# Four layers on one core, the last a mixture of experts: adds of two parts declared free of each other, weights kept, one list moved to the end

## The chip, the core and the metric

The kernel runs on one core of a Trainium2 chip. The metric is the device time of one execution in microseconds (us). Six kinds of engine matter here. TensorE (PE) multiplies matrices and turns tiles; VectorE (DVE), ScalarE (ACT) and GpSimd (POOL) compute on tiles; SyncE (SP) issues nearly all plain DMA transfers, from one queue, in order; GpSimd issues the indirect ones, which write rows to places that a list of numbers gives. Sixteen DMA engines move the data. Each engine works through its own instructions in the order in which the program emits them, and waits at an instruction until what it needs is there.

## What is computed

The input `x` has 16 sequences of 256 tokens of 256 numbers, in float32; `ctx` has the same shape. Four layers follow each other, each adding to `x`:

```
x = x + cross_attention_8_heads(ctx, layernorm(x))      # layer 1: keys from both, 512 of them
x = x + ffn_with_token_products(layernorm(x))           # layer 2: 1024 hidden, gelu
x = x + cross_attention_1_head(layernorm(x), ctx)       # layer 3
y = layernorm(x)                                        # layer 4: mixture of 8 experts
w = routing_weights(y @ Wr / temperature)               # 8 weights per token, some are 0
x = x + sum over e of w[e] * (silu(y @ Wg[e]) * (y @ Wu[e])) @ Wd[e]
```

An expert's three weights have 256 x 256 numbers each. A token counts for an expert only if its weight there is not 0.

## The kernel before

**Head loop.** The outer loop has 128 steps `n`, one for each head of each sequence (8 heads by 16 sequences), and two more to empty the pipeline. Step `n` computes scores `sc` (`s1`), then `pq` and `pk` of the next head, some filling work (`bulk`: values `pv`, the next sequence's input, and in the first sequence the loads of `load_late`), the product `po` of head `n-2` (`s3`), and the turning of the probabilities of head `n` (`s2`). The turning goes through memory: VectorE turns 32 x 32 blocks into `tb`, SyncE sends `tb` to a buffer `hop` in DRAM (L831) and, when that has landed, reads it back in another order as `pT` (L834). So `pT` of a head has to be back when `po` comes up two steps later.

**Chains.** What follows the first layer for one sequence is a generator, `chain`: output projection `px`, layer 2 (`ph`, `pf`), layer 3, and the last layernorm. Then `route` finds each token's experts and writes each row of the sequence into 8 lists in DRAM, `slots_d`, by 16 indirect DMAs on GpSimd (L638).

**Experts.** The sequences are split in two parts, of 9 and 7, so that the experts can start on the first part before the last sequences are done. A list of part 0 has 9 tiles of 128 rows for each expert, a list of part 1 has 7. They are worked in groups of 3, 3, 3 and of 4, 3 tiles (4, 2, 1 for the very last list): first all eight lists of part 0, then all eight of part 1. A group's rows are loaded from its list (L1040), turned through DRAM (L290, L296) into `yTd`, multiplied with the gate and up weights (`pg`, `pu`), and, in the midst of the next group, with the down weights (`pd`). VectorE scales each tile's result into `o` (8 buffers, L1122), and GpSimd adds it to the rows of the output in DRAM by an indirect DMA with addition (L1123). Rows of one list go to different places, so the adds of one list are declared free of each other by `apart`; adds of different lists wait for each other. A group's rows are loaded three groups ahead. For a group of part 1 that waits until `route` of the last sequence is through (the `ready` test).

**Weights.** `load_expert` loads the three weights of the expert two groups ahead (L1022 to L1024), into one of two buffers in turn, for each list anew: 16 loads.

**The order of the work** around the change is made by a planner at build time. `Clock.pe` is its estimate of TensorE's time; each matmul that is emitted moves it on. Chains, routes and experts are jobs in `line`; a job's `yield 2.5` says that its next unit is ready 2.5 us of clock later. Between the stages of the head loop, `gap` emits units of the first ready job until 0.8 us of clock are filled, and returns at once if no job is ready. After the head loop a last loop lets the clock jump to the next ready job until all are done.

**Memory.** Pools are opened and closed as stacks: `work_a` holds the head loop's tiles and `Wo_sb` to the end; `work_d`, the experts' tiles, is opened in the last step but two.

Of the kernel before, what the change touches and what calls it, by code (L numbers as in the profile page):

```python
# [12 lines left out]
F32 = mybir.dt.float32  # L13
# [16 lines left out]
def xattn_ffn_kernel(  # L30
# [74 lines left out]

    def apart(ins, group):
        tc.declare_no_dep(
            ins.ins, group=group, reason="rows of one group go to different places"  # L110
        )
        tc.add_to_no_dep_group(group, ins.ins)
        nc.gpsimd.nop()

    def gap(least=0.8):

        t = Clock.pe
        while Clock.pe - t < least:
            line[:] = [j for j in line if not j.done]
            job = next((j for j in line if j.ready <= Clock.pe), None)  # L120
            if job is None:
                return
            job.unit()
        line[:] = [j for j in line if not j.done]

# [529 lines left out]

    wh = ctx.enter_context(tc.tile_pool(name="work_a", bufs=2))
    with ExitStack() as sa, ExitStack() as sf:
        wi = sa.enter_context(tc.tile_pool(name="work_i", bufs=2))  # L660
        wf = sf.enter_context(tc.tile_pool(name="work_f", bufs=2, side="right"))

# [275 lines left out]
        def load_late(h):  # L938
            if h == 0:
                nats["W2"] = load_turn(W2, DC, HC, "W2e")  # L940
            if h == 1:
                nats["Wv"] = load_turn(Wv_w, DC, DC, "v1")
                nats["qk"] = load_fold()
            if h == 2:
                nc.sync.dma_start(Wo_sb, Wo.rearrange("(h p) d -> p h d", p=P))
                nc.sync.dma_start(Wr_sb, Wr.rearrange("(c p) e -> p c e", p=P))
                lasting["b2"] = row_everywhere(b2, "b2_bc")
                lasting["bv1"] = row_everywhere(Wv_b, "bv1_bc")
                lasting["scale"] = row_everywhere(ffn_scale, "scale_bc")
                lasting["invt"] = row_everywhere(temperature, "temp_bc")  # L950
            if h == 4:
                nc.vector.reciprocal(lasting["invt"], lasting["invt"])

        def all_turns():
# [49 lines left out]
        class D_:  # L1004


            w, wk = {}, None


        def open_front():  # L1010
            D_.front = ctx.enter_context(tc.tile_pool(name="front_d", bufs=2, side="right"))

        def open_last_layer():
            D_.wk = ctx.enter_context(tc.tile_pool(name="work_d", bufs=2))

        def load_expert(key):
            e = key[1]
            k = len(D_.w) % 2
            w = D_.w[key] = (D_.wk if k else D_.front).tile(
                [P, 3, DC, D], F32, tag=f"wx{k}", bufs=1, name=f"wx_{key[0]}_{e}"  # L1020
            )
            nc.sync.dma_start(w[:, 0], Wg[e].rearrange("(c p) i -> p c i", p=P))  # L1022
            nc.sync.dma_start(w[:, 1], Wu[e].rearrange("(c p) i -> p c i", p=P))
            nc.sync.dma_start(w[:, 2], Wd[e].rearrange("(c p) d -> p c d", p=P))  # L1024

        class G:


            def __init__(self, part, e, t0, tiles, more):
                self.part, self.e, self.tiles = part, e, tiles  # L1030
                self.key = (f"{part}{more}", e)
                self.name = f"{part}_{e}_{t0}"
                self.first = e * NTOKS[part] + t0 * P

# [45 lines left out]

            def gate(self, i):
                n = self.tiles * P
                w = D_.w[self.key]
                if i == 0:
                    self.hT = D_.wk.tile(
                        [P, IC, n], F32, tag="hTd", name=f"hTd_{self.name}",
                        padded_shape=[P, IC, NG],
                    )
                self.pg = mm_tile(n, f"pg_{self.name}_{i}")
                for d in range(DC):  # L1090
                    mm(
                        self.pg, w[:, 0, d, ts(i, P)], in_order(self.yT)[:, d],
                        start=(d == 0), stop=(d == DC - 1),
                    )
                self.sg = D_.wk.tile(
                    [P, n], F32, tag="sg", name=f"sg_{self.name}_{i}", padded_shape=[P, NG]
                )
                nc.scalar.activation(self.sg, self.pg, AF.Tanh, scale=0.5)  # L1098

            def up(self, i):  # L1100
                w, sg = D_.w[self.key], self.sg
                pu = mm_tile(self.tiles * P, f"pu_{self.name}_{i}")
                for d in range(DC):
                    mm(
                        pu, w[:, 1, d, ts(i, P)], in_order(self.yT)[:, d],
                        start=(d == 0), stop=(d == DC - 1),
                    )
                nc.vector.scalar_tensor_tensor(sg, sg, 1.0, self.pg, ALU.add, ALU.mult)
                nc.vector.tensor_tensor(self.hT[:, i, :], sg, pu, ALU.mult)  # L1109

            def down(self, t):
                if t >= self.tiles:
                    return
                w = D_.w[self.key]
                pd = mm_tile(D, f"pd_{self.name}_{t}")
                for i in range(IC):
                    mm(
                        pd, self.hT[:, i, ts(t, P)], w[:, 2, i, :],
                        start=(i == 0), stop=(i == IC - 1),
                    )  # L1120
                o = D_.wk.tile([P, D], F32, tag="o", bufs=8, name=f"o_{self.name}_{t}")
                nc.vector.tensor_scalar(o, pd, self.wt[:, t : t + 1], None, ALU.mult)  # L1122
                ins = nc.gpsimd.indirect_dma_start(  # L1123
                    out=out_rows[0 : sum(NTOKS[: self.part + 1]), :],
                    out_offset=bass.IndirectOffsetOnAxis(ap=self.at[:, t : t + 1], axis=0),
                    in_=o, in_offset=None, compute_op=ALU.add,
                )
                apart(ins, f"out_{self.part}_{self.e}")

        def experts(groups, ready=None):  # L1130

            load_expert(groups[0].key)
            for g in groups[:2]:
                g.load()
            yield 7.0
# [6 lines left out]
            for n, g in enumerate(groups):  # L1142
                if n == 0:
                    groups[2].load()
                if n + 3 < len(groups):
                    while ready is not None and not ready(groups[n + 3]):
                        yield 0.4
                for i in range(IC):
                    g.gate(i)
                    yield  # L1150
                    g.up(i)
                    yield
                    if n == 0:
                        groups[1].turn_rows(i)
                    if n + 2 < len(groups):
                        if i == 0:
                            groups[n + 2].send_rows()
                        else:
                            groups[n + 2].fetch_rows()
                    if i == 0 and n + 3 < len(groups):  # L1160
                        groups[n + 3].load()
                    if late is not None:
                        late.down(2 * i)
                        late.down(2 * i + 1)
                        yield
                if n + 2 < len(groups) and groups[n + 2].key not in D_.w:
                    load_expert(groups[n + 2].key)
                late = g
            for t in range(late.tiles):
                late.down(t)  # L1170

        def groups(part, more, sizes, last_sizes=None):

            gs = []
            for e in range(E):
                t = CAPS[part] // P if more else 0
                for k in last_sizes if last_sizes and e == E - 1 else sizes:
                    gs.append(G(part, e, t, k, more))
                    t += k
                assert t == NTOKS[part] // P if more else t == CAPS[part] // P  # L1180
            return gs

        last = None
        for n in range(NS + 2):
# [6 lines left out]
            if n == NS - 4:  # L1191
                sf.close()
                open_front()
                rest = Job(experts(
                    groups(0, "", (3, 3, 3)) + groups(1, "", (4, 3), (4, 2, 1)),
                    lambda g: g.part == 0 or last.tail.done,
                ))
                line.append(rest)
# [2 lines left out]
                open_last_layer()  # L1201
            while behind_exp:
                behind_exp.pop()()
            gap()
            if n < NS:
                s1_scale(n)
            if n + 1 < NS:
                s0q(n + 1)
            gap()
            if n + 1 < NS:  # L1210
                s0k(n + 1)
            gap()
            advance(more)
            gap()
            advance(more)
            gap()
            if n >= 2:
                s3(n - 2)
            gap()
            if n < NS:  # L1220
                s2(n)
        line.remove(rest)
# [2 lines left out]
        while line:  # L1225
            while behind_exp:
                behind_exp.pop()()
            if not any(j.ready <= Clock.pe for j in line):
                Clock.pe = min(j.ready for j in line)
            gap()  # L1230


        more_d = keep.tile([P, 2, E], F32, name="more_d")
# [46 lines left out]
```

## Time and profile before

| what | value |
|---|---|
| median of 3 runs | 1898.36 us (1895.84 to 1899.13) |
| the profiled execution, its own time | 1899.3 us |
| its span | 1897.6 us |
| TensorE busy (matmul) | 1845.4 us, 97% |
| VectorE, ScalarE, GpSimd busy | 1179.6, 594.8, 872.3 us |
| mean granted TensorE clock | 0.991 |
| bytes moved by DMA | 309.89 MB, 163 GB/s |
| GpSimd's adds to the output (L1123) | 128, 1562 ns each |
| GpSimd's writes of slots (L638) | 256, 1050 ns each |
| matmuls of the experts pg, pu, pd | 127.6, 125.3, 123.8 us |
| last layer's groups, first pg to last pd | 1477.7 to 1877.9 us |

The span is the time from the first to the last recorded instruction; the execution's own time is 1.7 us longer. Busy time of one engine can lie beside that of another, so the shares don't add up to one. In the lines of the timelines that follow, the first number is the start in us from the start of the span, the second the duration, then the engine, the source line, the operation and the tiles (what is written <- what is read), how many instructions are merged in the line, and in brackets how long the engine had been idle before and what ended that. Matmuls overlap by a fraction of a microsecond, so the start of the next line says more than the end of one.

### The profile page before, as it was taken

To read this page: it belongs to the slowest core of one execution; us is meant where nothing else is said; L and a number is where in the kernel's file an instruction comes from. 1 tells how busy PE (TensorE), PEld (TensorE's weight loads), DVE (VectorE), ACT (ScalarE), POOL (GpSimd) and SP (SyncE) were. 2 spreads that over 40 slices of the span, in tenths; PEclk is the share of its full clock that TensorE was granted. 3 is DMA by queue.
4 is the path that set the end of the run, shared out by engine and by line. 5 is a ranking of instruction groups with operands and counts; after the bars stand their busy time and mean duration, and the time that the engine had idled before them with its cause. 6 is when DMAs were issued, how large, how long until landed. Compare 5 with 4: busy or idle time off the path is not lost.

```text
span 1897.6 us, 22669 instructions
## 1 busy us (share of the span) xinstructions
PE 1845.4 (97%) x6822; PEld 1252.6 (66%) x6822; DVE 1179.6 (62%) x3211; ACT 594.8 (31%) x1309; POOL 872.3 (46%) x996
## 2 busy tenths in 40 slices
PE   8999999999999999999999999999999999999995
PEld 4566666666666666666666666667676767665554
DVE  5356667666666666666675766666657476656553
ACT  3333434343333333333333333333333221111110
POOL 3122353535353535353534444444434367766565
PEclk9999999999999999999999999999999999999998
DMA  6553445454545444444454444444435477999995
GB/s 217 160 170 103 161 137 159 141 166 138 162 140 159 148 151 157 151 147 149 146 160 151 149 154 143 159 140 160 142 118 177 135 200 194 250 234 241 249 220 96
DMA packets 235083, 309.89 MB, mean 163 GB/s; under 512 B 27036, under 2 KB 195912, under 8 KB 232904
## 3 DMA queue, kind: packets, MB, share of 16 engines
q1 hardware_dynamic: 204184, 256.80, 43.2%
q0 software_dynamic: 30720, 51.54, 11.5%
q8 instruction: 57, 0.93, 0.2%
q14 instruction: 74, 0.61, 0.1%
q10 hardware_dynamic: 48, 0.01, 0.0%
HBM read 157.51 MB, written 150.73 MB: 162 GB/s over the span
## 4 chain that ended last, share of the span: by engine, by line
PE 90%; DVE 3%; DMA 2%; ACT 2%; POOL 1%; issue 1%; SPq 1%; ACTq 0%; POOLq 0%; DVEq 0%
PE po L83 13%; PE pv L83 13%; PE sc L83 12%; PE pk L83 10%; PE pq L83 7%; PE px L83 6%; PE pf L83 6%; PE ph L83 5%; PE pg L83 5%; PE pu L83 5%; PE pd L83 5%; ACT pr L810 1%; DMA wx<-in_L_ffn_Wg_dram 1%; DVE tb L827 1%; POOL out_dram L1123 1%
## 5 line engine op out<-in xcount | busy, mean ns | idle before, releaser
L818 POOL TENSOR_SCALAR pr<-pr,ri 128x512 f32<-128x512 f32 x256 | 183.9, 726 | 478.9 <-DVE ri L817 477.4
L810 ACT ACTIVATE pr<-sc,nm 128x512 f32<-128x512 f32 x256 | 173.8, 683 | 506.2 <-DVE nm L804 505.8
L638 POOL DMA_INDIRECT slots_d<-row,at_slot x256 | 268.7, 1050 | 121.6 <-DVE at_slot L634 64.8
L1123 POOL DMA_INDIRECT out_dram<-o,at x128 | 200.0, 1562 | 128.7 <-DMA out_dram<-o,at 37.8
L83 PE MATMUL po<-pT,v 128*128 128x256 f32 x1024 | 246.9, 385 | 8.9 <-DMA pT<-hop 8.9
L83 PE MATMUL sc<-kT,qT 128*128 128x512 f32 x512 | 241.5, 594 | 0.9 <-ACT kT L743 0.9
L83 PE MATMUL pk<-kvT,Wk_sb 128*128 128x512 f32 x512 | 240.7, 592 | 0.0
L83 PE MATMUL pv<-Wv_sb,kvT 128*128 128x512 f32 x512 | 238.6, 595 | 0.0
L83 PEld LDWEIGHTS po<-pT,v 128*128 128x128 f32 x1024 | 194.2, 192 | 63.2 <-issue 28.4
L804 DVE TENSOR_REDUCE nm<-sc 128x1 f32<-128x512 f32 x256 | 162.1, 666 | 16.9 <-PE sc L83 16.9
L827 DVE STREAM_TRANSPOSE tb<-pr 128x512 f32<-128x512 f32 x256 | 165.3, 683 | 7.2 <-DMA hop<-tb 7.2
L851 DVE TENSOR_SCALAR outT<-po,cvec 128x256 f32<-128x256 f32 x128 | 60.8, 475 | 164.3 <-PE po L83 164.3
L83 PEld LDWEIGHTS pv<-Wv_sb,kvT 128*128 128x128 f32 x512 | 96.0, 190 | 95.1 <-issue 89.2
L83 PEld LDWEIGHTS sc<-kT,qT 128*128 128x128 f32 x512 | 97.5, 191 | 69.4 <-issue 61.5
L83 PEld LDWEIGHTS pk<-kvT,Wk_sb 128*128 128x128 f32 x512 | 97.5, 190 | 68.0 <-issue 61.2
L1098 ACT ACTIVATE sg<-pg 128x384 f32<-128x384 f32 (+3 forms) x82 | 41.3, 504 | 312.3 <-PE pg L83 299.3
L83 PE MATMUL pg<-yTd,wx 128*128 128x384 f32 (+3 forms) x328 | 127.6, 512 | 11.2 <-DMA wx<-in_L_ffn_Wg_dram 7.0
L83 PE MATMUL pq<-kvT,Wq_sb 128*128 128x256 f32 x512 | 132.5, 381 | 0.0
L83 PE MATMUL pu<-yTd,wx 128*128 128x384 f32 (+3 forms) x328 | 125.3, 505 | 0.3 <-DVE hT L427 0.2
L83 PE MATMUL pd<-wx,hTd 128*128 128x256 f32 x512 | 123.8, 379 | 0.2 <-DVE hTd L1109 0.2
L83 PE MATMUL ph<-ybT,W1e 128*128 128x256 f32 x512 | 121.4, 380 | 0.1
L83 PEld LDWEIGHTS pq<-kvT,Wq_sb 128*128 128x128 f32 x512 | 96.6, 191 | 36.7 <-issue 22.7
(197 smaller groups left out, 2685.9 us busy)
## 6 DMA issues: line engine op xcount, KB each, us to landing
hop<-tb SPq DMA_DIRECT2D x128, 512.0 KB
pT<-hop SPq DMA_DIRECT2D x512, 128.0 KB
ev<-ev_d SPq DMA_DIRECT2D x16, 1024.0 KB
rows<-slots_d SPq DMA_DIRECT2D x31, 397.5 KB
hop_rows_b<-rows_b SPq DMA_DIRECT2D x29, 384.0 KB
yTd<-hop_rows_b SPq DMA_DIRECT2D x116, 96.0 KB
rows<-slots_d SPq DMA_DIRECT2D x8, 530.0 KB
cin<-in_ctx_dram SPq DMA_DIRECT2D x16, 256.0 KB
```

Source lines behind the costliest of these rows:

```text
L83: nc.tensor.matmul(out, lhsT, rhs, **kw)
L638: ins = nc.gpsimd.indirect_dma_start(out=slots_d[part], out_offset=bass.IndirectOffsetOnAxis(ap=at_slot[:, c, e : e + 1], axis=0), in_=row ...
L804: nc.vector.tensor_reduce(nm, sc, AX.X, ALU.max, negate=True)
L810: nc.scalar.activation(pr, sc, AF.Exp, bias=nm, accum_out=sm)
L818: nc.gpsimd.tensor_scalar(pr, pr, ri, 1.0, ALU.mult, ALU.mult)
L827: nc.vector.transpose(tb[:, :, c, :], heads[n][c][0].rearrange("p (m f) -> p m f", m=QP))
L851: nc.vector.tensor_scalar(A.outT[b][:, h, :], po, col("bv", h), None, ALU.add)
L1098: nc.scalar.activation(self.sg, self.pg, AF.Tanh, scale=0.5)
L1123: ins = nc.gpsimd.indirect_dma_start(out=out_rows[0 : sum(NTOKS[: self.part + 1]), :], out_offset=bass.IndirectOffsetOnAxis(ap=self.at[:, ...
```

## The change

It has five pieces.

1. `apart` declares an add free also of all adds of the other part, whose rows are other rows of the output.
2. The order of the lists: experts 0 to 6 of part 0, experts 0 to 6 of part 1, expert 7 of part 0, expert 7 of part 1. So the first group of part 1 is number 21 of the order, where it was 24.
3. `load_expert` loads each expert once: the first into `front_d`, the second into `work_d`, the other six into a new pool `weights_d`. That takes the place of `work_a`, which is closed when the last sequence's output projection has been emitted; until then the experts' job stands still if it wants a third expert. `work_d` goes to the right side.
4. `gap` has a new argument `stand`: if no job is ready, but one will be within so much clock, the clock is moved there and the job goes on. It is 2.0 in the last three steps of the head loop, 0 before, and without a limit in the last loop.
5. Six loads of the first sequence (`Wo_sb`, `Wr_sb`, two biases, a scale, the temperature) move from head 2 to head 5, and the reciprocal of the temperature from head 4 to head 7.

```diff
-    def apart(ins, group):
-        tc.declare_no_dep(
-            ins.ins, group=group, reason="rows of one group go to different places"
-        )
+    def apart(ins, group, others=()):
+        for g in (group, *others):
+            tc.declare_no_dep(
+                ins.ins, group=g, reason="rows of one group go to different places"
+            )
         tc.add_to_no_dep_group(group, ins.ins)
         nc.gpsimd.nop()
-    def gap(least=0.8):
+    def gap(least=0.8, stand=0.0):
         t = Clock.pe
         while Clock.pe - t < least:
             line[:] = [j for j in line if not j.done]
+            if not line:
+                return
             job = next((j for j in line if j.ready <= Clock.pe), None)
             if job is None:
-                return
+                soon = min(j.ready for j in line)
+                if soon > Clock.pe + stand:
+                    return
+                Clock.pe = soon
+                continue
             job.unit()
...
-            if h == 2:
+            if h == 5:
                 nc.sync.dma_start(Wo_sb, Wo.rearrange("(h p) d -> p h d", p=P))
                 nc.sync.dma_start(Wr_sb, Wr.rearrange("(c p) e -> p c e", p=P))
                 lasting["b2"] = row_everywhere(b2, "b2_bc")
...
-            if h == 4:
+            if h == 7:
                 nc.vector.reciprocal(lasting["invt"], lasting["invt"])
...
-            D_.wk = ctx.enter_context(tc.tile_pool(name="work_d", bufs=2))
+            D_.wk = ctx.enter_context(tc.tile_pool(name="work_d", bufs=2, side="right"))
+        def open_rest():
+            D_.more = ctx.enter_context(tc.tile_pool(name="weights_d", bufs=1))
-        def load_expert(key):
-            e = key[1]
-            k = len(D_.w) % 2
-            w = D_.w[key] = (D_.wk if k else D_.front).tile(
-                [P, 3, DC, D], F32, tag=f"wx{k}", bufs=1, name=f"wx_{key[0]}_{e}"
-            )
+        def load_expert(e):
+            k = len(D_.w)
+            pool = D_.front if k == 0 else D_.wk if k == 1 else D_.more
+            w = D_.w[e] = pool.tile([P, 3, DC, D], F32, bufs=1, name=f"wx_{e}")
...
-                apart(ins, f"out_{self.part}_{self.e}")
+                apart(
+                    ins, f"out_{self.part}_{self.e}", [f"out_{1 - self.part}_{e}" for e in range(E)]
+                )
...
-                if n + 2 < len(groups) and groups[n + 2].key not in D_.w:
-                    load_expert(groups[n + 2].key)
+                if n + 2 < len(groups) and groups[n + 2].e not in D_.w:
+                    while len(D_.w) > 1 and D_.more is None:
+                        yield 0.4
+                    load_expert(groups[n + 2].e)
...
+        lists = (
+            groups(0, "", (3, 3, 3), range(E - 1)) + groups(1, "", (4, 3), range(E - 1))
+            + groups(0, "", (3, 3, 3), [E - 1]) + groups(1, "", (4, 2, 1), [E - 1])
+        )
...
-            gap()
+            stand = 2.0 if n >= NS - 1 else 0.0
+            gap(stand=stand)
...
-            if not any(j.ready <= Clock.pe for j in line):
-                Clock.pe = min(j.ready for j in line)
-            gap()
+            if D_.more is None and B - 1 in A.projected:
+                sh.close()
+                open_rest()
+            gap(stand=1e9)
```

## The prediction

> **What bounds the kernel now.** I read the page's slices first: TensorE's row is full nearly everywhere, so only a hole in that row, or the time after the last matmul, can be won.
>
> ```profile
> PE   8999999999999999999999999999999999999995
> DMA  6553445454545444444454444444435477999995
> ```
>
> Each digit is a fortieth of the span (47 us). TensorE is below 9 only in the first slice and the last; the DMA engines are at 9 in the last layer. The table by 50 us stretches then gives TensorE's busy time: the losses lie in 50-100 us (45.57 of 50), 1450-1500 (44.98), 1550-1600 (47.14), from 1700 on, and in the tail. I opened the timelines there.
>
> *Start.* TensorE's timeline (start, duration, tile, what it waited for):
>
> ```profile
> 55.15 1.88 PE L83 MATMUL pv<-Wv_sb,kvT 128*128 128x512 f32 x4
> 61.46 3.75 PE L83 MATMUL po<-pT,v 128*128 128x256 f32 x8 [4.43 <-DMA pT<-hop]
> ```
>
> The head's product po waits 4.43 us for pT, and then takes 3.54 us to the next instruction (65.00) instead of the 1.72 it takes elsewhere; the sc behind it takes 2.29 instead of 1.72. The hole is 4.43 + 1.82 + 0.57 = 6.8 us. SyncE's timeline tells why pT is late:
>
> ```profile
> 43.67 0.82 SPq L945 DMA_DIRECT2D Wo_sb<-in_L_xattn_Wo_dram  x1
> ...
> 48.03 3.51 SPq L296 DMA_DIRECT2D raw<-hop_cin  x4
> ...
> 54.01 0.38 SPq L831 DMA_DIRECT2D hop<-tb  x1
> 56.96 1.74 SPq L834 DMA_DIRECT2D pT<-hop  x4
> ```
>
> The six late loads are issued from 43.67 to 47.98, the transposed inputs behind them to 53.43, and only then the head's hop, although its tb was finished by VectorE at 43.26.
>
> *End of the head loop.* The same wait, for the last heads, as nothing is emitted between two po:
>
> ```profile
> 1474.13 3.75 PE L83 MATMUL po<-pT,v 128*128 128x256 f32 x8 [4.52 <-DMA pT<-hop]
> 1477.68 2.25 PE L83 MATMUL pg<-yTd,wx 128*128 128x384 f32 x4
> ```
>
> 4.52 us here and 0.50 just before; po takes 3.55 to the next start instead of 1.73, pg and pu 2.08 and 1.29 instead of 1.29 each. Together 5.0 + 1.8 + 0.8 = 7.6 us.
>
> *Second part.* TensorE at the start of two experts, and the sum of its waits from 1640 to 1880:
>
> ```profile
> 1796.68 1.96 PE L83 MATMUL pg<-yTd,wx 128*128 128x512 f32 x4 [1.92 <-DMA wx<-in_L_ffn_Wg_dram]
> ...
> 1836.67 2.78 PE L83 MATMUL pg<-yTd,wx 128*128 128x512 f32 x4 [2.76 <-DMA wx<-in_L_ffn_Wg_dram]
> 1839.25 2.79 PE L83 MATMUL pu<-yTd,wx 128*128 128x512 f32 x4
> ```
>
> ```profile
> PE pg L83 <- DMA wx<-in_L_ffn_Wg_dram: 7.0, 5, 2.8
> ```
>
> A seven-tile expert takes 18.07 us when nothing is late (1758.46 to 1776.53). The eight start at 1721.81, 1740.32, 1758.46, 1776.53, 1796.68, 1815.61, 1836.67, 1856.52: the seven periods exceed 18.07 by 0.44, 0.07, 0, 2.08, 0.86, 2.99, 1.78, in sum 8.2 us. With the hole before the first (1719.87 to 1721.81) it is 10.2 us, of which 0.9 belongs to a wait for o (0.62 us at 1815.61), the rest to weights.
>
> *Tail.* GpSimd's timeline, its last adds:
>
> ```profile
> 1853.04 1.54 POOL L1123 DMA_INDIRECT out_dram<-o,at  x1 [0.30 <-DVE o L1122]
> 1860.32 1.54 POOL L1123 DMA_INDIRECT out_dram<-o,at  x1 [5.74 <-DVE sg L1108]
> ...
> 1875.88 1.54 POOL L1123 DMA_INDIRECT out_dram<-o,at  x1 [2.92 <-DVE o L1122]
> ...
> 1886.97 1.54 POOL L1123 DMA_INDIRECT out_dram<-o,at  x1 [0.30 <-issue]
> ```
>
> Adds follow each other at 1.85 us, but the first add of an expert stands until the last of the expert before has landed: 5.74 us here, 5.5 to 6.8 at the six full boundaries in part 2. Its period, 6 x 1.85 + 1.54 + wait, was 18.2 to 19.5 us, longer than TensorE's 18.07. The last matmul ends at 1877.9, the last o at 1878.40, the last add begins at 1886.97; 9.1 us after that instruction the span ends.
>
> **The change, part by part.**
>
> *Late loads from h=2 to h=5: 6.6 us gained.* Six DMAs (Wo, Wr, two biases, scale, temperature), all on SyncE, 4.31 us of issue. Taken from the old place, hop can be issued at about 48.2-49.7, pT 2.95 us later (as 54.01 to 56.96), landed some 4.5 us after that (56.96 to 61.46): 55.7-57.2, while TensorE comes to po at 57.03. So 6.6 to 6.8; I take 6.6 and keep 4.4 as the lower end. In the new place they are moved past the hop and pT of head 4; SyncE has nothing from 71.64 to 77.00, 5.36 us for 4.31 us of issue. Queued behind is the hop of head 5, whose pT was landed about 84 and needed at 93.57: 9 us of cover, which must be spent before this costs anything. The reciprocal moved to h=7 is 0.14 us on VectorE, which idles there for 5 us. GpSimd's queue holds none of them.
>
> *Standing clock in the last three iterations: 3.7 us gained.* The planner may now let its clock run until a job is ready, so expert work goes between the last heads. sc ends at 1466.34; the second rowsT still waits for the copy of the first (ended 1468.95), and the first pg for the second copy, about 1470.1. That leaves 2.3 + 0.75, say 3.0 us, open; then the first expert, po (its pT lands near 1474) and the rest follow closed. For slowed matmuls behind such a hole I charge 0.9: 7.6 - 3.0 - 0.9 = 3.7. Ends: 7.6 (other jobs fill it) and -3 (the experts' row loads come ahead of the last head's hop on SyncE, rows_b ahead of its tb on VectorE, and po of the last head waits). The last sequence's px starts later, by up to what was moved ahead, some 7 us.
>
> Here a rule weighs in. The Trainium skill, "TensorE: Matmul & The Clock Gate", in its section on the HAM clock gate, says the clock halves only after a whole idle window of about 3.4 us. By that the 3.0 us hole costs nothing more, and the gain were 4.6. The row at 1836.67 says otherwise: after 2.76 us idle the two groups took 5.21 us to the next start instead of 3.44, while after 1.92 us (1796.68) they took 3.51. I follow the row.
>
> *Weights kept: 9.2 us gained.* Eight of the 16 loads go away: 8 x 3 issues on SyncE and 8 x 768 KB (6.3 MB; the DMA engines there were busy for 0.92 to 1.00 of the time). All weight waits of the second part go, 10.2 - 0.9 = 9.3; the o wait is dealt with below; and one list of part 0 still meets a fresh load, where such starts cost 0.2-0.5 (1647.55, 1695.86): -0.5. The o wait's own 0.9 goes half with the lag of the adds: +0.4. Sum 9.2. What is late next is yTd, fetched a group ahead (1789.09 for a start at 1806.2), then o with 8 buffers. Ends 4 (the adds set the period, see rival) and 10.2. The pool for six experts opens when the last px is emitted; expert 2 is wanted at group 4's end (1541), px ended at 1500: 41 us of cover. The wait lies in the planner's line, not on an engine; the load's wait for the old buffers' readers is over by 1500 as well. Behind it on SyncE stand hops of rows.
>
> *Adds free across parts, last list of part 0 held back: 6.1 us gained, the tail.* In the order 0:e0-6, 1:e0-6, 0:e7, 1:e7 the first adds of each of the last two lists find their forerunners long landed, as do those of 1:e0: 15 waits become 12. The nine adds of 0:e7 take 16.65 us, TensorE needs 3 x 7.75 = 23.25: GpSimd makes up 6.6 us of lag, plus the wait saved. It was some 9 us late at 1860.32 (first o of that list about 1851.5). If it has caught up, the seven last adds begin 0.55 after the first o is ready (1869.25), one every 1.85: 1869.8 to 1880.9 instead of 1886.97, 6.1 us. Ends 0 and 6.1; no more, since the pace is the instruction's. GpSimd's queue order is otherwise kept, no new wait is added, the nop per add stays.
>
> The second rule: "DMA: Bandwidth & Descriptors", section on the anatomy of a GpSimd DMA, gives about 2.0 us fixed per DMA, mostly the landing, plus bytes: estimate 2.3 us for an add of 128 KB. Then remaining boundaries would shrink from 5.7 to 2.3, the period from 18.2 to 14.9, and no lag could arise. The rows: 5.5-6.8 with full DMA engines, but 2.92 at 1875.88, where they are half idle (0.45). The second part loses about 18% of its bytes, so I take 4.5-5.5: period 17.1-18.1, just not the bound. Both ends give the same sum here; the row alone leaves room for the rival.
>
> *Middle, 1500-1720: 0.* Its 4.9 us of holes (2.16 at 1564.43 for o, and slow matmuls behind) come from a GpSimd queue with adds and slot writes; experts earlier could spread or crowd it: -5 to +4.9, and no row decides. The removed If-loads cost nothing: the branch isn't taken.
>
> **Sum.** 6.6 + 3.7 + 9.2 + 6.1 = 25.6. From the profiled execution, 1899.3 (span 1897.6), 1873.7; the median of the runs is 0.9 lower: 1872.8, so 1873.
>
> **Rivals.**
> - *The adds set the pace* (0.2). Period stays 18.9: seven lists of the second part lose 0.8 each, 5.6 us, and half the tail, 3: 25.6 - 8.6, 1881. For it: 18.2-19.5 in the rows; against: 2.92 when unloaded.
> - *The loop's end gets worse* (0.1). -3 in place of 3.7: 1880.
> - *The declaration does nothing* (0.06): as before 15 waits, no catching up, tail kept: 1879.
> - *More is won in the middle and at the loop's end* (0.1): 1864.
> - *Slower: the last routing comes too late* (0.04). With one list held back, the first rows of part 2 are wanted three groups, 23 us, sooner: at the load of group 18, which before was
>
> ```profile
> 1678.45 0.44 SPq L1040 DMA_DIRECT2D rows<-slots_d  x1
> ```
>
> while the last slot write was
>
> ```profile
> 1659.24 0.96 POOL L638 DMA_INDIRECT slots_d<-row,at_slot  x1 [0.30 <-issue]
> ```
>
> Landed by 1668 with the longest landing of an add, 8.2. The margin is 10 us; px is put back about 7, the gap closed 4: it just holds. Beyond it, SyncE stands with yTd behind it, VectorE's rows_b next, and TensorE loses one for one after about 8 us more (a group of 7.75). Slower begins at a delay of 10 + 8 + 25.6 = 44 us; with 50 it were 1904. Three iterations of six gaps can put ahead at most 18 x 1.29 = 23 us.
>
> **Chances.** Likeliest case, 1867 to 1878: 0.5. A measurement here tells about 0.2% (3.8 us) from no change. Faster 0.93, within 0.2% 0.03, slower 0.04. Range 1862 to 1886: it takes in the rivals but the last, and leaves about 2 in 10 out at its ends.
>
> **What would show it.** Step 1: no wait at the third po near 57, everything after 6.6 us earlier. Step 2: pg before the po of head 125 and a hole of about 3 us near 1462. Step 3: no wait for wx after the first part, periods of 18.1. Step 4: the last add 3 us after the last matmul. Wrong would be: GpSimd's lag still 9 us at the held list; a wait for rows at group 18; a hole at po of the last head.

## The result, and the profile after

| | before | after |
|---|---|---|
| median | 1896.41 us (1888.46 to 1899.13, 6 runs) | 1869.18 us (1868.18 to 1870.94, 6 runs) |
| the profiled execution | 1899.3 us, span 1897.6 | 1868.18 us, span 1866.4 |
| TensorE busy | 1845.4 us, 97% | 1833.6 us, 98% |
| mean granted TensorE clock | 0.991 | 0.998 |
| bytes moved by DMA | 309.89 MB | 303.60 MB |

The ratio is 0.9861 (95%: 0.9843 to 0.988): 27.2 us less, where 25.6 were forecast. The two profiled executions lie 31.1 us apart, since that of before was 2.9 us above the median of its runs and that of after 1.0 below. The page's slices of the kernel after:

```profile
PE   8999999999999999999999999999999999999997
DMA  6553535454545454445454545454534667999986
```

TensorE's row is full to the last slice, whose digit rose from 5 to 7. In the last layer the row of the DMA engines still shows 9, until two slices before the end; closer, their share is 0.96 from 1740 to 1840 in the kernel before and 0.88 from 1700 to 1800 in this one, both within the second part. Where the 31.2 us of span came from, by points that both traces have:

| stretch | before | after | gain |
|---|---|---|---|
| start to `sc` of the last head | 1464.63 | 1457.12 | 7.5 |
| to the first `pg` of group 18 (the last list of experts 0 to 6, part 0) | 207.44 | 198.85 | 8.6 |
| to the end of the last matmul | 205.8 | 196.9 | 8.9 |
| to the end of the span | 19.7 | 13.5 | 6.2 |

*Start.* TensorE's timeline of after, at the third `po`, and SyncE's beside it:

```profile
56.35 1.89 PE L83 MATMUL po<-pT,v 128*128 128x256 f32 x8
58.08 1.88 PE L83 MATMUL sc<-kT,qT 128*128 128x512 f32 x4
```

```profile
48.01 0.38 SPq L840 DMA_DIRECT2D hop<-tb  x1
51.15 1.74 SPq L843 DMA_DIRECT2D pT<-hop  x4
...
65.89 0.44 SPq L954 DMA_DIRECT2D Wo_sb<-in_L_xattn_Wo_dram  x1
...
69.50 0.33 SPq L840 DMA_DIRECT2D hop<-tb  x1
74.28 0.80 SPq L843 DMA_DIRECT2D pT<-hop  x2
```

The `hop` stands at 48.01 where it stood at 54.01, so `pT` is issued at 51.15 and `po` begins at 56.35 with no wait and runs at its usual 1.73. In their new place the six loads hold SyncE from 65.89 to 69.2. The `hop` behind them starts at 69.50 and its `pT` 4.8 us later instead of some 3, probably because it shares the DMA engines with the loads (no run tries that); no `po` waits for it.

*End of the head loop*, TensorE's timeline:

```profile
1461.56 0.55 PE L87 MATMUL rowsT<-ident,rows 128*128 128x128 f32 x3 [2.23 <-ACT yTd L750]
1461.94 1.64 PE L83 MATMUL pg<-yTd,wx 128*128 128x384 f32 x4
...
1464.71 1.89 PE L83 MATMUL po<-pT,v 128*128 128x256 f32 x8
...
1472.78 0.91 PE L83 MATMUL pg<-yTd,wx 128*128 128x384 f32 x2 [2.29 <-DVE yTd L754]
```

and VectorE's, the copy for which the last of these waits:

```profile
1472.17 0.55 DVE L754 COPY yTd<-rowsT 128x384 f32<-128x384 f32 x1
```

The first `pg` and `pu` now stand ahead of the `po` of head 125 (1464.71). That `po` doesn't wait any more, nor do the two that follow (1477.83 and 1488.62). The hole before the second `rowsT` is 2.23. A second one, of 2.29, is in no sum of the prediction: VectorE's queue holds the transposition of the next rows (`rows_b`, 1468.87), which waited 1.42 us for them, then the last head's `tb`, then a group's `sg` and `hTd`, and only at 1472.17 the copy to `yTd` that `pg` needs. The prediction had this queue among its lower ends, as a wait of `po`; it hit `pg`.

*Second part and tail.* The two longest sums of TensorE's waits from 1640 to 1860 (us in total, times, longest), and GpSimd's last adds (the add now stands at L1132):

```profile
PE pu L83 <- DVE o L1131: 1.8, 1, 1.8
PE pg L83 <- DMA yTd<-hop_rows_b: 0.2, 1, 0.2
```

```profile
1812.58 1.56 POOL L1132 DMA_INDIRECT out_dram<-o,at  x1 [5.57 <-DMA out_dram<-o,at]
...
1825.56 1.54 POOL L1132 DMA_INDIRECT out_dram<-o,at  x1 [0.31 <-issue]
...
1844.54 1.54 POOL L1132 DMA_INDIRECT out_dram<-o,at  x1 [1.05 <-DVE o L1131]
...
1855.63 1.54 POOL L1132 DMA_INDIRECT out_dram<-o,at  x1 [0.30 <-issue]
```

No matmul of the last layer waits for weights any more. A new wait has come in, 1.84 us for a free `o` at 1659.26, in the last list before part 1. The lists of part 1 start at 1681.72, 1699.86, 1717.93, 1736.00, 1754.07, 1772.14 and 1790.21, the held list at 1808.28: periods of 18.07, but the first, 18.14. In the 100 us from 1700 TensorE is busy for 100.00. The add at 1812.58 is still a boundary (5.57); the held list begins at 1825.56 with no such wait. At the first add of the last list (1844.54), as at the add before it (1841.95), it is GpSimd that waits for `o`: it has caught up. The last add starts 2.7 us after the last matmul ends (1852.91), where it was 9.1.

### The profile page after: what moved, and what is told of

Same layout as the page of the kernel before. It is cut to its first block, busy times and chain, and to the rows that moved or that the text cites. A ratio compares the mean times of both kernels' runs of the same rounds, so it can differ in the third digit from the quotient of the medians.

```text
span 1866.4 us, 22620 instructions
## 1 busy us (share of the span) xinstructions
PE 1833.6 (98%) x6822; PEld 1249.3 (67%) x6822; DVE 1179.0 (63%) x3211; ACT 594.3 (32%) x1309; POOL 870.5 (47%) x996
## 2 busy tenths in 40 slices
DMA packets 228555, 303.60 MB, mean 163 GB/s; under 512 B 26652, under 2 KB 189384, under 8 KB 226376
## 4 chain that ended last, share of the span: by engine, by line
PE 90%; DVE 4%; ACT 2%; DMA 2%; POOL 1%; issue 1%; SPq 0%; ACTq 0%; DVEq 0%; POOLq 0%
PE po L83 13%; PE pv L83 13%; PE sc L83 12%; PE pk L83 10%; PE pq L83 7%; PE ph L83 6%; PE px L83 6%; PE pf L83 6%; PE pd L83 5%; PE pu L83 5%; PE pg L83 5%; ACT pr L819 1%; DVE tb L836 1%; PE pl L83 1%; DMA out_dram<-o,at 1%
## 5 line engine op out<-in xcount | busy, mean ns | idle before, releaser
L1132 POOL DMA_INDIRECT out_dram<-o,at x128 | 199.8, 1561 | 114.0 <-issue 31.0
L750 ACT COPY v<-pv 128x512 f32<-128x512 f32 x100 | 58.5, 585 | 197.4 <-PE pv L83 197.4
```

Of the source, the lines that this page charges most:

```text
L750: nc.scalar.copy(out, src)
L1132: ins = nc.gpsimd.indirect_dma_start(out=out_rows[0 : sum(NTOKS[: self.part + 1]), :], out_offset=bass.IndirectOffsetOnAxis(ap=self.at[:, ...
```

## The experiments

Each kernel is the changed one with one thing edited, unless said otherwise, and was timed beside the kernel before on its chip. The changed kernel stands at 1869.18 in the first series; a second one beside the later kernels gave 1871.45 (0.9874, 0.9852 to 0.9897). That is a little above the 1867 to 1871 that were expected of it. So what an edit costs is known to about 2 us at best, and I give it against both; for `u_free_order`, `u_weights` and `o11` the second is the nearer, as it is from the same chip. The 95% intervals of the ratios are wider still, some 4 us each way, and all below but that of `w_only` overlap with that of the second series. What each edit does is therefore read from its trace.

**u_loads**, the six loads back at head 2:

```diff
-            if h == 5:
+            if h == 2:
...
-            if h == 7:
+            if h == 4:
```

> The changed kernel with the six late loads back at head 2 and the reciprocal at head 4. Mine: the third po waits about 4.4 us for pT again and runs slow after it, nothing later makes it good, so 6.6 us slower than the changed kernel, about 1876. Rival (the loop has slack and regains what is lost at its start): within 2 us of the changed kernel, 1869 to 1871.

Measured: 1877.38 us, ratio 0.9901 (0.9881 to 0.992), 8.2 above the changed kernel (5.9 above its second series). TensorE's timeline:

```profile
61.90 3.75 PE L83 MATMUL po<-pT,v 128*128 128x256 f32 x8 [4.49 <-DMA pT<-hop]
65.45 2.35 PE L83 MATMUL sc<-kT,qT 128*128 128x512 f32 x4
```

The wait of 4.49, the `po` of 3.55 to the next start and the slowed `sc` are all back, as in the kernel before. What is lost at 60 us is not regained in the 1800 us behind it: the step's 6.6 holds.

**u_stand**, no standing clock in the last steps of the loop:

```diff
-            stand = 2.0 if n >= NS - 1 else 0.0
+            stand = 0.0
```

> The changed kernel with the clock not standing in the last three steps (stand 0). From the last head's sc to group 18 the change won 8.6 us where 3.7 had been forecast. Mine: all of it hangs on the experts' early start, which closes the hole before po of the last heads and also spreads GpSimd's queue, so that the hole for o in the middle stays away: 8 us slower, about 1877, with both holes back. Rival: only the loop's end hangs on it, 3 us, about 1872, and the middle is better for another reason (weights that wait for no buffer).

Measured: 1875.24 us, ratio 0.989 (0.9871 to 0.991), 6.1 above (3.8), between the 8 and the 3 of the two theories. The stretch from the last head's `sc` to the first list of part 1 is 230.8 us instead of 224.6 (226.0 in the second series). TensorE's timeline:

```profile
1466.70 3.75 PE L83 MATMUL po<-pT,v 128*128 128x256 f32 x8 [4.57 <-DMA pT<-hop]
...
1555.04 1.70 PE L83 MATMUL pg<-yTd,wx 128*128 128x384 f32 x4 [2.14 <-DVE o L1131]
```

Both the hole at `po` and the one for `o` in the midst of the experts, 88 us later, come back with this one line. So the middle's loss belonged to the late start of the experts, and the forecast of 0 for it was too cautious.

**u_free**, adds of the two parts not declared free of each other, order of lists as in the change:

```diff
-                apart(
-                    ins, f"out_{self.part}_{self.e}", [f"out_{1 - self.part}_{e}" for e in range(E)]
-                )
+                apart(ins, f"out_{self.part}_{self.e}")
```

> The changed kernel with apart as before: adds of the two parts wait for each other. Mine: the held list's first add waits for the landing of list 1:e6 (some 5.5 us), list 1:e7 for that of the held list (3 to 5 us), 8 us at the tail, about 1877 (1875 to 1880). Rival: the nine tiles of the held list give enough room for the adds to catch up with the waits, only 2 us, 1871.

Measured: 1875.25 us, ratio 0.9891 (0.9872 to 0.991), 6.1 above (3.8). GpSimd's timeline:

```profile
1831.98 1.54 POOL L1132 DMA_INDIRECT out_dram<-o,at  x1 [4.66 <-DMA out_dram<-o,at]
...
1851.38 1.54 POOL L1132 DMA_INDIRECT out_dram<-o,at  x1 [3.05 <-DVE hTd L1118]
...
1862.47 1.54 POOL L1132 DMA_INDIRECT out_dram<-o,at  x1 [0.30 <-issue]
```

Two waits that the change doesn't have: 4.66 at the held list's first add, 3.05 at the first of the last list. The last add starts 7.9 us after the last matmul (1854.6) instead of 2.7, which is 5.2 of the 6.6 us by which the span is longer.

**u_order**, the old order of lists, adds declared free:

```diff
-            groups(0, "", (3, 3, 3), range(E - 1)) + groups(1, "", (4, 3), range(E - 1))
-            + groups(0, "", (3, 3, 3), [E - 1]) + groups(1, "", (4, 2, 1), [E - 1])
+            groups(0, "", (3, 3, 3), range(E)) + groups(1, "", (4, 3), range(E - 1))
+            + groups(1, "", (4, 2, 1), [E - 1])
```

> The changed kernel with the lists in the old order (all of part 0, then all of part 1), adds of the parts still declared free. Mine: the last list waits for the one before it and GpSimd is late at the end, the tail after the last matmul grows by about 5 us: 1874 (1872 to 1875). Rival: with the weights' traffic gone the adds land fast enough and the order is worth 1 us or less, 1870.

Measured: 1874.68 us, ratio 0.9892 (0.9871 to 0.9913), 5.5 above (3.2). GpSimd's last adds, and TensorE about the border of the parts:

```profile
1845.24 1.54 POOL L1132 DMA_INDIRECT out_dram<-o,at  x1 [1.71 <-DVE o L1131]
1849.80 1.54 POOL L1132 DMA_INDIRECT out_dram<-o,at  x1 [3.02 <-DVE sg L1117]
```

```profile
1699.73 1.53 PE L83 MATMUL pg<-yTd,wx 128*128 128x384 f32 x4 [1.42 <-DVE sg L1117]
```

The size is near what I expected, the reason only half: GpSimd was not late at the end, as at 1845.24 it waits for `o`. The single boundary at 1849.80 costs 3.02, and the last add (1860.89) comes 4.7 us after the last matmul: 2.0 more than in the change. Another 2.8 us are waits of TensorE at the border of the parts: this 1.42, and 0.83 and 0.54 for `o` at 1682.54 and 1708.25. The nearest reading is that the extra list of part 0 there, with 9 adds and its boundary, keeps the `o` buffers full; no run tries that by itself, and in the next run, with the same order, the longest wait there is another, 1.89 us for the weights of the eighth expert.

**u_free_order**, both edits together:

> The changed kernel with both taken back, the free adds and the held list; weights kept. Alone they cost 6.1 (free adds) and 5.5 us (order) against the changed kernel. Mine: both act on the same thing, the adds' lag at the last lists, so together less than the sum: 8 us, 1877. Rival: they are independent, 11.6 us, 1881.

Measured: 1877.26 us, ratio 0.9909 (0.9885 to 0.9933), 8.1 above (5.8), less than 6.1 + 5.5; by the second series it is less than 3.8 + 3.2 too, but by no more than the noise. The first and the last add of the last list:

```profile
1853.30 1.54 POOL L1132 DMA_INDIRECT out_dram<-o,at  x1 [2.95 <-DVE hTd L1118]
...
1864.39 1.54 POOL L1132 DMA_INDIRECT out_dram<-o,at  x1 [0.30 <-issue]
```

The last matmul ends at 1856.4, 3.5 us later than in the change, and the last add starts 8.0 us after it. With the two runs above, that gives the way from the last matmul to the last add for all four cases:

| | old order | one list moved to the end |
|---|---|---|
| adds of the parts wait for each other | 8.0 us | 7.9 us |
| adds of the parts free | 4.7 us | 2.7 us |

Moving the list takes nothing off this way as long as the adds wait. Freeing them helps in either order: in the old one it frees the boundary between the parts, and from there GpSimd catches up. In `u_order` it waits for `o` in each of the six lists that follow the first of part 1 (0.57 to 1.71 us), while here it waits at each boundary for adds to land (2.95 to 5.75 us) and never for `o`. All periods of TensorE in the second part, but the first (18.14), are 18.07 here too, although every boundary waits, so the adds don't set its pace.

**u_weights**, weights loaded for each list, two buffers, as in the kernel before:

```diff
-        def load_expert(e):
-            k = len(D_.w)
-            pool = D_.front if k == 0 else D_.wk if k == 1 else D_.more
-            w = D_.w[e] = pool.tile([P, 3, DC, D], F32, bufs=1, name=f"wx_{e}")
+        def load_expert(key):
+            e = key[1]
+            k = len(D_.w) % 2
+            w = D_.w[key] = (D_.wk if k else D_.front).tile(
+                [P, 3, DC, D], F32, tag=f"wx{k}", bufs=1, name=f"wx_{key[0]}_{e}"
+            )
...
```

> The changed kernel with the weights loaded for each list anew into two buffers in turn, 16 loads as before. Mine: the waits for weights come back in the second part (9 us there), 1878 (1876 to 1881), with periods between 18.1 and 21 us, and the adds land later. Rival (the waits came from the lag of the adds, which the free adds take away): only 3 us, 1872.

Measured: 1878.28 us, ratio 0.9905 (0.9881 to 0.9928), 9.1 above the first series (6.8 above the second, of the same chip). TensorE's waits from 1640 on:

```profile
PE pg L83 <- DMA wx<-in_L_ffn_Wg_dram: 6.5, 6, 1.5
```

Against none in the change. From the first list of part 1 to the last matmul it takes 6.75 us more than the change, about as much as these waits. The tail is not touched (2.7 us again): the weights are worth their waits.

**w_only**, the other way round: the kernel before with nothing but the kept weights (loads at head 2, old order, adds not free, no standing clock in the last steps; its diff from before is the third piece, and the way in which the last loop moves the clock):

> The kernel before with the weights kept and nothing else of the change (loads at head 2, no standing clock, adds as before, old order). Mine: the weight waits of the second part go, its periods are 18.1, and the adds, though each list waits for the one before, do not hold TensorE up, as in the run without free adds and with the old order: 9 us faster than before, 1887. Rival (the adds' period of 18.2 to 19.5 us takes the place of the weights): periods near 18.9, 4 us faster, 1892.

Measured: 1888.77 us, ratio 0.9951 (0.9931 to 0.9972), 9.4 below the kernel before beside it. TensorE starts the lists of part 1 at 1721.02, 1739.16, 1757.23 and on to 1847.58, every 18.07 from the second on. One of GpSimd's boundaries in it:

```profile
1743.74 1.54 POOL L1132 DMA_INDIRECT out_dram<-o,at  x1 [5.45 <-DMA yTd<-hop_rows_b]
```

It waits 5.45, the next two 5.36 at 1761.73 and 5.62 at 1779.98, and their period (18.0 and 18.2) is as long as TensorE's. That is as near as the rival "the adds set the pace" came: after a wait of 0.68 for `o` at the first list, no list's start shows one.

**o11**, eleven buffers for `o` instead of eight, against the 1.84 us hole at 1659:

```diff
-                o = D_.wk.tile([P, D], F32, tag="o", bufs=8, name=f"o_{self.name}_{t}")
+                o = D_.wk.tile([P, D], F32, tag="o", bufs=11, name=f"o_{self.name}_{t}")
```

> The changed kernel with 11 buffers for o instead of 8. Mine: the hole of 1.84 us for o at group 18 is gone and GpSimd's lag there hurts nobody: 2 us faster than the changed kernel, 1867. Rival: GpSimd's queue is late there whatever the buffers, the hole only moves: 1869.

Measured: 1868.02 us, ratio 0.9854 (0.9829 to 0.988), beside 0.9874 (0.9852 to 0.9897) for the changed kernel: 3.4 us below its second series, 1.2 below its first. The hole is gone, but three others (0.56, 0.53, 0.67) stand near it, as the rival had it in part. The loop's end happened to take 2.6 us longer than in the second series in its profile (a hole of 3.04 with slowed matmuls behind it). From the last `po` but one (1479.78) to the first list of part 1 (1683.75) it takes 204.0 us, where the changed kernel took 205.5 in its second series and 203.9 in its first. A gain of 2 us is neither shown nor excluded.

## Why the prediction was right, point by point

The pieces undone cost 8.2 (loads), 6.1 (clock), 8.1 (free adds and order together) and 9.1 (weights), in sum 31.5 by the first series and 22.3 by the second (5.9, 3.8, 5.8, 6.8); the change measured 27.2 and 23.8 beside them. That the sum of 25.6 came within 1.6 us of the measured 27.2 is luck in part: by the traces the terms came to 31.2, and the two profiled executions lie 3.9 us farther apart than the medians.

- *Late loads, 6.6.* 7.5 up to the last head, 6.9 of it at the third `po`; undone 8.2 or 5.9. Right. The cover in the new place held.
- *Standing clock, 3.7, and the middle, 0.* This is the term that was mis-sized. The stretch gained 8.6. TensorE's idle time in it fell from 9.1 us (207.44 - 198.31 busy) to 6.6, and its busy time from 198.31 to 192.21 for the same matmuls: 6.1 us, most of it from those that no longer run slowed (some 4 us at the `po` of 1474.13 and at the `o` hole of 1564.43). The granted clock of the stretch went from 0.98 to 1.00. At the loop's end the forecast of one hole of 3.0 with 0.9 for slowed matmuls met 2.23 + 2.29 with 0.3: a gain of about 3. Another 3 lie in the middle, where the hole for `o` and the slow matmuls behind it (4.9) are gone and smaller waits (0.36, 1.26, 0.51) stand. The excess over 3.7 is then 4.9, of which `u_stand` confirms a part: the standing clock undone lengthens the same stretch by 6.5 us (7.0 by the second series), and the way to the first list of part 1 by 6.2 (4.7). The rival "more is won in the middle" (1864) had the right sign and some half of its size (4.9 of 9).
- *Weights, 9.2.* The second part gained 8.9; alone they gave 9.4, undone they cost 9.1 or 6.8. Right, though the 8.9 is what remains after a loss that stood in no sum, the wait of 1.84 for `o` at 1659.26, where the kernel before waited 0.29. It isn't the work of the kept weights, as u_weights has waits at the same place (1.50 and 0.53); what brought it stays open. The lower end (4, the adds' pace) is refuted by w_only.
- *Free adds and the held list, 6.1.* The tail gained 6.2. Right. The landing waits were put at 4.5 to 5.5 with less traffic; they measured 4.5 to 6.2 in the second part of after, and 3.8 to 4.4 in the middle of u_order's, where GpSimd was not late. The busy share of the DMA engines fell only from 0.96 (1740 to 1840 before) to 0.88 (1700 to 1800 after). The estimate of 2.3 from the rule of "DMA: Bandwidth & Descriptors" that was weighed is not reached in any wait that I read; the least were 2.92 before, at 1875.88, and 2.95 in u_free_order at 1853.30, both at the emptied end. Since TensorE took 18.07 either way, this decided nothing; the held list's 23.25 us of matmuls did.
- *The clock's rule against the row.* The rule of the Trainium skill ("TensorE: Matmul & The Clock Gate", HAM clock gate) would have every hole under some 3.4 us free of more; after 2.14 us in u_stand and in w_only the matmuls were slow, so the row was nearer. But neither is a price: 2.23 and 2.29 us idle cost some 0.3 together in the change, where the row let me charge 0.9, and in four other profiles the same 2.23 cost about 1.5 (last section).
- *Slower, the last routing.* The last slot write ended at 1655.6, and the rows of the first list of part 1 were loaded at 1664.07, 8.5 us later. Routing did not set that time: the slot writes from 1640 on landed 3.7 to 6.3 us after their issue, and SyncE shows no wait for them. The load stood behind the rows of the group before (1663.63), which came late from VectorE, as VectorE had stood 5.79 us for a free `o` (until 1658.72). `yTd` was then 0.21 late at 1681.72. So it held, with some 3 us to spare; one list more held back would want these rows three groups sooner and has no such margin.
- *The other rivals.* That the declaration does nothing is refuted by u_free (two waits and 5.2 us of tail come back) and, in the old order, by u_order beside u_free_order; that the loop's end gets worse, by the rows at 1461 to 1473, though its mechanism, VectorE held by the next rows, is there and costs up to 2.29.

The second hole at the loop's end is 0.59 us in four profiles (u_loads, u_free, u_weights, the second series of the change) and 2.2 to 3.0 in four (after, u_order, u_free_order, o11). The first hole explains it: in just the first four its 2.23 us are followed by slowed `pg` and `pu`, so TensorE comes later to the second, which VectorE's copy ends: the `pg` behind it starts 15.4 to 15.7 us after the `sc` in six of the eight (16.1 and 16.4 in u_free_order and o11). Slowed or not, the `po` behind it starts 20.4 to 20.7 us after the `sc` in these six. So slowed matmuls cost nothing here, as TensorE would have waited for VectorE anyway.

Still open: nearly 3 us of the gain from the last `sc` to group 18, spread over matmuls and short waits, that I can't put at one place; and what decides whether a hole is followed by slowed matmuls.

## What to carry to other kernels

Before costing a change in the last layer, divide the loss into holes of the bounding engine and slowed work behind them: here the matmuls' own time was 6.1 of the 8.6 us that one stretch gave back, and filling a hole early removed another 88 us later. Judge together a declaration that frees transfers of each other and an order that puts such transfers side by side: here the order alone took 0.1 us off the tail, the declaration alone 3.3, and both 5.3. A load that is needed late should be issued behind the next deadline on its queue, since on an in-order queue what is urgent behind it waits out its issue time (here six loads and the inputs behind them, and 4.4 us of wait at one `po`).

## What the runs showed of the hardware that I had not expected

The same idle time of TensorE, for the same wait at the same place, slowed what followed in one profile and not in another. TensorE's timeline in the second series of the changed kernel:

```profile
1660.02 2.63 PE L83 MATMUL pu<-yTd,wx 128*128 128x384 f32 x4 [2.37 <-DVE o L1131]
...
1664.83 1.45 PE L83 MATMUL pg<-yTd,wx 128*128 128x384 f32 x4
```

And in u_loads:

```profile
1667.77 1.56 PE L83 MATMUL pu<-yTd,wx 128*128 128x384 f32 x4 [2.37 <-DVE o L1131]
...
1670.95 1.56 PE L83 MATMUL pg<-yTd,wx 128*128 128x384 f32 x4
```

2.37 us idle in both; from the end of it to the next group 4.81 us in the one, at a mean granted clock of 0.65, and 3.18 in the other, at 1.00. The first hole at the loop's end shows it in all eight profiles with the standing clock: 2.23 us before the second `rowsT` each time, but in four of them what follows is slowed. In the second series of the changed kernel (beside the lines of after above):

```profile
1462.18 0.75 PE L87 MATMUL rowsT<-ident,rows 128*128 128x128 f32 x3 [2.23 <-ACT yTd L750]
1462.72 2.77 PE L83 MATMUL pg<-yTd,wx 128*128 128x384 f32 x4
```

From the end of the hole to the `po` of head 125 it takes 4.66 us here, at a mean clock of 0.63, and 3.15 in after, at 1.00. If the clock is at half while it is down (0.50 is what the trace of u_stand gives for its `po` behind the hole of 4.57, from 1466.70 to 1470.24), these means come to about 3.4 us at half speed in both places, an estimate: (1 - 0.65) / 0.5 x 4.81 and (1 - 0.63) / 0.5 x 4.66. So such a hole costs about 1.7 us on top of itself or next to nothing.

In w_only 2.14 us idle were followed by slowed matmuls (`pg` 2.47, `pu` 2.28), in u_free_order 2.77 were not, in o11 3.04 were. So from 2.14 to 3.04 us an idle time cost up to 1.8 us on top of itself or next to nothing, and its length alone doesn't tell which. The page of the Trainium skill named above also says that the window in which the hardware counts runs freely; where a hole lies in it may be what differs, but no run here shows that. Of those that I read, none of up to 1.92 us did it and each of 4.43 and more did (a `po` of 3.75). A forecast should carry both ends for each such hole, and ask what waits behind it: at the loop's end the slowed matmuls cost nothing, since the next `pg` waited for VectorE either way.
